# A four-layer graph network on one core: the first batch's opening chain by chunks, the order of the first loads, and the way in which column scales become rows

## The chip, the core and the metric

The kernel runs on one core of a Trainium2 chip. The metric is the device time of one execution in microseconds (us). The kernel before took 2319.86 us, the median of 3 runs (2318.74 to 2319.90).

The engines of the core are named as the profile names them: PE (matrix products; PEld is its load of the stationary operand), DVE (vector work), ACT (activation functions and copies), POOL (general work on the side, here mostly `x ** -0.5`), SP (here: the queue that starts the transfers). They run side by side, each through its own list of instructions in a fixed order, and wait for each other by semaphores. All data is float32.

## What is computed

For each of 32 batches there is a node matrix `x` of 512 x 128 and an adjacency matrix of 512 x 512. Four layers follow each other; each normalises its input, clips it at zero, and adds a graph network of that to the input:

```python
# layer 0
h = maximum(layernorm(x), 0)
d = sum(adj + I, axis=-1);  r = d ** -0.5
x = x + leaky_relu((r[:, None] * (adj + I) * r[None, :]) @ (h @ W) + b, 0.01)
# layer 1
h = maximum(layernorm(x), 0)
x = x + tanh(concat(adj @ elu(h @ W_in + b_in), elu(h @ W_node + b_node),
                    adj.T @ elu(h @ W_out + b_out)) @ W_upd + b_upd)
# layer 2: four inner layers over f, with the same two normalised matrices in all four
h = maximum(layernorm(x), 0)
A1 = adj / sqrt(sum(adj**2, axis=2));  A2 = adj / sqrt(sum(adj**2, axis=1))
f = tanh(concat(A1 @ (f@ws + bs), f@wn + bn, A2.T @ (f@wd + bd)) @ wu + bu)     # four times
x = x + f
# layer 3: a gated update (tanh of adj @ msg, then gates r, z, n)
```

What matters below: layer 0 can't start before the row sums of the batch's adjacency matrix and the mean and variance of its `x` are known. Layer 2 needs the square root of the sum of squares of each row and of each column of the matrix.

## The kernel before

A batch's matrix is held twice, as `a` (rows on the partitions, four chunks of 128 x 512) and as `aT` (its transpose). Instructions aren't written in the order in which they run. Every operation is recorded with an estimated duration, and a list scheduler (`Plan.order`) then fixes the order on every engine: among the operations that are ready it takes the one with the smallest key. The key comes from the batch's due time and the length of what still follows. A `rank` puts an operation ahead of all that have none. The estimates decide the order only; the hardware waits on semaphores.

```python
plan = Plan(sb, psum, {"bank": 8, "s2": 32, "s4": 6, "s8": 10}, {...})    # buffers of each size
o.key = (due - o.tail + o.later if o.rank is None else o.rank - 1e6, i)
def t_pow(n): return 0.9 + 0.1 * n          # estimate for the power on POOL
```

Where the plan expects PE to stand idle for over 0.7 us, it puts in products of the identity matrix with itself, into a bank that nobody uses ("idle products", tile `ps_idle`). They compute nothing that is needed[...].

```python
def kept_warm(self, done, product, begin):
    ...
        gap = o.ready - at
        if gap > self.SHORT:
            n = int(min(gap, cold) / self.COLD + max(gap - cold - 0.1, 0.0) / self.WARM)
```

The loads of the setup and of the first batch, with their ranks (a small one goes first). `raw` holds layer 2's weights, which the kernel multiplies together once at the start ("fold") so that the inner layers get by with fewer products:

```python
op("AQ", ..., w_sb[:, :D] ...)                      # layer 0's weight, on ACT's queue
op("AQ", ..., r_sb[:, :D] ...)                      # layer 0's bias, on ACT's queue
op("SP", 0.5, ... c_sb, bcol ..., rank=2)
op("SP", 0.5, ... w_sb[:, D:first] ..., rank=5)
op("SP", 0.5, spread(D, R_L3_MSG), ..., rank=5)
... raw[...] ..., rank=3 if i == 0 else 6           # three pieces: 768, 768 and 576 KB
def load(dst, src, kb, rank):                       # 4 pieces for batch 0, else 2
    ... rank=None if b else rank
op("SP", 0.4, ... xt.ap(), x[b] ..., rank=None if b else 0)
load(a, adj[b], 1024, 1)
load(aT, adjt[b], 1024, 4)
```

Layer 0's opening. `degree` sums the rows of `a` on ACT, the power is taken of all eight columns at once, and every chunk of `h` waits for all of it:

```python
def normed(xin, out_tag, extra=None):
    mv = moments(xin, v8)                                   # DVE: mean, variance of x
    if extra: extra(v8); n = 2 * NC                         # degree: row sums
    op("POOL", t_pow(n), ... inv[:, :n] = v8[:, :n] ** -0.5)
    op("DVE", 0.08, ... inv[:, at:at+NC] = inv[:, 0:NC] * inv[:, NC:2*NC])
    op("DVE", 0.08, ... nb = -mean * inv)
    for c in range(NC):
        op("ACT", ..., h[:, c, :] = relu(x[:, c, :] * inv[c] + nb[c]))

def degree(v8):
    for c in range(NC):
        op("ACT", 0.73, ... activation(sq, a[:, c, :], AF.Copy, accum_out=stat[:, c:c+1]))
    op("DVE", 0.08, ... v8[:, NC:] = stat + 1.0)

hr, inv0 = normed(xt, "h", degree)
def own(k, n):                                              # adds the identity to aT's own blocks
    nc.gpsimd.tensor_tensor(diag[:, k:k+n, :], blocks, ident..., op=ALU.add)
n = NC if b else 1
... op("POOL", ...)
psh = plan.bank("agg")                                      # then PE: aT and diag times h
```

After it come, for each batch, a copy of the aggregate (ACT), the product with layer 0's weight (`ps_lin`), `z`, `y` and the new `x` (DVE), the next normalisation, a transpose (`ps_t`), layer 1's two projections (`ps_sd`), their elu (`rep`, ACT and DVE), and layer 1's aggregation (`ps_agg<-aT,rep`).

Layer 2's scales. The sums of squares stand one for each partition; the multiplication of `aT` and `a` needs them along a row, the same on every partition. So they go to DRAM and come back spread over all partitions, as (node, scale), and ACT puts them into rows:

```python
inv = buf("inv", (P, 2 * NC))
op("POOL", t_pow(2 * NC), ... inv = stat ** -0.5)
bounce, spaced, rows = buf("bounce", (P, 2*NC)), buf("s4", (P, P, 2*NC), "spaced"), buf("s4", (P, 2, N), "rows")
op("SP", 0.4, bounced, [inv], [bounce], kb=128)             # 4 KB to DRAM
op("SP", 0.4, spread, [bounce], [spaced], kb=512)           # back, to every partition
op("ACT", t_act(2 * N), ... copy rows "p (s c) n" from spaced "p k n")
for s, m in enumerate((aT, a)):
    for c in range(NC):
        op("DVE", t_tt(N), ... m[:, c, :] = m[:, c, :] * rows[:, s, :])
```

Of the kernel before, what the change touches and what calls it, by code (L numbers as in the profile page):

```python
# [18 lines left out]
P = 128  # L19
# [5 lines left out]
PERIOD = 30.0  # L25
ENDING = 6.0
SMALL = 16


SEVEN = {"last": 0 * 5 * D, "mid": 1 * 5 * D, "gates": 2 * 5 * D}  # L30
# [9 lines left out]
W_L2 = []  # L40
# [219 lines left out]
def gnn_stack(  # L260
# [13 lines left out]
    sb = ctx.enter_context(tc.tile_pool(name="sb", bufs=1))  # L274
    psum = ctx.enter_context(tc.tile_pool(name="psum", bufs=1, space=bass.MemoryType.PSUM))
    dram = ctx.enter_context(tc.tile_pool(name="dram", bufs=1, space=bass.MemoryType.DRAM))
    plan = Plan(sb, psum, {"bank": 8, "s2": 32, "s4": 6, "s8": 10}, {"bank": 2, "s2": 5, "s4": 0, "s8": 1})

    w_sb = const.tile([P, W_COLS], F32, name="w_sb")
    c_sb = const.tile([P, C_COLS], F32, name="c_sb")  # L280
# [2 lines left out]
    cf_sb = const.tile([P, len(L2_CHUNKS)], F32, name="cf_sb")  # L283
    t_sb = const.tile([P, T_COLS], F32, name="t_sb")
    ident = const.tile([P, P], F32, name="ident")
    neg_half = const.tile([P, 2 * NC], F32, name="neg_half")

    def wt(col, n=D):
# [18 lines left out]
    def t_pool(n):  # L307
        return 0.15 + n / 450

    def t_pow(n):  # L310
        return 0.9 + 0.1 * n

    def op(*args, **kwargs):
        return plan.op(*args, **kwargs)

    def const_buf(name, ap):
        b = Buf(plan, name, name, None)
# [3 lines left out]
    W1, W2F, W3, CS, RS, RF, CF, TS, ID, NH = (const_buf(n, t) for n, t in (  # L321
        ("w1", w_sb), ("w2", w_sb), ("w3", w_sb), ("c_sb", c_sb), ("r_sb", r_sb), ("rf_sb", rf_sb),
        ("cf_sb", cf_sb), ("t_sb", t_sb), ("ident", ident), ("neg_half", neg_half)))

    def mm(ps, out_of, lhs, rhs, n, start, stop, reads, later=0.0):
        op("PE", t_mm(n), lambda: nc.tensor.matmul(out_of(ps.ap()), lhs(), rhs(), start=start, stop=stop),  # L326
# [10 lines left out]
    def setup():  # L337
# [1 line left out]

        op("POOL", 1.0, lambda: make_identity(nc, ident), [], [ID])  # L340
        op("POOL", 0.2, lambda: nc.gpsimd.memset(neg_half, -0.5), [], [NH])
        first = W_L2[0][0]

        def spread(lo, hi, to=None):
            return lambda: nc.sync.dma_start(
                r_sb[:, lo:hi] if to is None else to.ap()[:, :hi - lo], bass.AP(tensor=brow.tensor, offset=brow.offset + lo, ap=[[0, P], [1, hi - lo]]))
# [2 lines left out]
        op("AQ", 0.5, lambda: nc.scalar.dma_start(w_sb[:, :D], w[:, :D]), [], [(W1, {0})], kb=64)  # L349
        op("AQ", 0.5, lambda: nc.scalar.dma_start(  # L350
            r_sb[:, :D], bass.AP(tensor=brow.tensor, offset=brow.offset, ap=[[0, P], [1, D]])), [], [(RS, {0})], kb=64)
        op("SP", 0.5, lambda: nc.sync.dma_start(c_sb, bcol), [], [CS], kb=9, rank=2)
        op("SP", 0.5, lambda: nc.sync.dma_start(w_sb[:, D:first], w[:, D:first]), [], [(W1, {1})], kb=(first - D) / 2, rank=5)
        op("SP", 0.5, spread(D, R_L3_MSG), [], [(RS, {1})], kb=(R_L3_MSG - D) / 2, rank=5)
        op("SP", 0.5, spread(R_L3_MSG, R_COLS), [], [(RS, {2})], kb=(R_COLS - R_L3_MSG) / 2)
        hrz = plan.buf("s2", (P, N), "hrz")
        op("SP", 0.5, spread(R_L3_HRZ, R_L3_HRZ + 2 * D, hrz), [], [hrz], kb=D)
# [3 lines left out]
        for i in (0, 2, 3):  # L361
            lo, hi = RAW_L2[i][0], RAW_L2[i + 1][0] if i == 2 else RAW_COLS if i == 3 else RAW_L2[2][0]
            buf = plan.buf("s8", (P, NC, N), f"raw{i}")
            op("SP", 0.5, lambda buf=buf, lo=lo, hi=hi: nc.sync.dma_start(
                buf.ap().rearrange("p c n -> p (c n)")[:, :hi - lo], raw[:, lo:hi]), [], [buf], kb=(hi - lo) / 2, rank=3 if i == 0 else 6)
            raws += [(buf, lo)] * (2 if i == 0 else 1)
        op("SP", 0.5, lambda: nc.sync.dma_start(w_sb[:, W_L3_MSG:], w[:, first:]), [], [W3], kb=(W_COLS - W_L3_MSG) / 2)

        def block(i, col):
            buf, lo = raws[i]  # L370
# [48 lines left out]
    def program(b):  # L419
        plan.batch = b  # L420

        def buf(tag, shape=(P, N), name=None):
            return plan.buf(tag, shape, name)
# [10 lines left out]

        def load(dst, src, kb, rank):

            n = NC // pieces
            for k in range(pieces):
                s = slice(k * n, (k + 1) * n)
                op("SP", 0.4, lambda s=s: nc.sync.dma_start(dst.ap()[:, s, :], src[:, s, :]),  # L440
                   [], [(dst, set(range(NC)[s]))], kb=kb / pieces, rank=None if b else rank)

        op("SP", 0.4, lambda: nc.sync.dma_start(xt.ap(), x[b]), [], [xt], kb=256, rank=None if b else 0)
        load(a, adj[b], 1024, 1)
        load(aT, adjt[b], 1024, 4)

        def moments(xin, v8):
            st, mv = buf("bn", (P, NC, nc.vector.BN_STATS_DIM)), buf("mv", (P, NC, nc.vector.BN_AGGR_DIM))
            for c in range(NC):
                op("DVE", 0.193, lambda c=c: nc.vector.bn_stats(st.ap()[:, c, :], xin.ap()[:, c, :]), [xin], [(st, {c})])  # L450
            for c in range(NC):
                op("DVE", 0.066, lambda c=c: nc.vector.bn_aggr(mv.ap()[:, c, :], st.ap()[:, c, :]), [(st, {c})], [(mv, {c})])
            op("DVE", 0.08, lambda: nc.vector.tensor_scalar_add(v8.ap()[:, 0:NC], mv.ap()[:, :, 1], LN_EPS), [mv], [(v8, {0})])  # L453
            return mv

        def normed(xin, out_tag, extra=None):


            v8 = buf("v8", (P, 2 * NC))
            n = NC  # L460
            mv = moments(xin, v8)
            if extra:
                extra(v8)
                n = 2 * NC
            inv = buf("sc", (P, 3 * NC))
            op("POOL", t_pow(n), lambda: nc.gpsimd.tensor_tensor(inv.ap()[:, :n], v8.ap()[:, :n], neg_half[:, :n], op=ALU.pow),  # L466
               [v8, NH], [(inv, {0})])
            at = 0
            if extra:
                at = 2 * NC  # L470
                op("DVE", 0.08, lambda: nc.vector.tensor_mul(inv.ap()[:, at:at + NC], inv.ap()[:, 0:NC], inv.ap()[:, NC:2 * NC]),
                   [(inv, {0})], [(inv, {1})])
            nb = buf("nb", (P, NC))
            op("DVE", 0.08, lambda: nc.vector.scalar_tensor_tensor(nb.ap(), mv.ap()[:, :, 0], -1.0, inv.ap()[:, at:at + NC],  # L474
                                                                   op0=ALU.mult, op1=ALU.mult), [mv, inv], [nb])
            h = buf("s2", rows_shape, out_tag)
            for c in range(NC):
                op("ACT", t_act(D, 2), lambda c=c: nc.scalar.activation(  # L478
                    h.ap()[:, c, :], xin.ap()[:, c, :], AF.Relu, bias=nb.ap()[:, c:c + 1],
                    scale=inv.ap()[:, at + c:at + c + 1]), [xin, nb, inv], [(h, {c})])  # L480
            return h, inv
# [157 lines left out]
                    sq.ap(), a.ap()[:, c, :], AF.Copy, accum_out=stat.ap()[:, c:c + 1]), [(a, {c})], [sq, (stat, {c})])  # L639
            op("DVE", 0.08, lambda: nc.vector.tensor_scalar_add(v8.ap()[:, NC:], stat.ap(), 1.0), [stat], [(v8, {1})])  # L640

        hr, inv0 = normed(xt, "h", degree)

        diag = buf("s2", rows_shape, "diag")

        def own(k, n):
            t = aT.ap()
            blocks = bass.AP(tensor=t.tensor, offset=t.offset + k * (N + P), ap=[list(t.ap[0]), [N + P, n], [1, P]])
            nc.gpsimd.tensor_tensor(diag.ap()[:, k:k + n, :], blocks, ident[:, None, :].to_broadcast([P, n, P]), op=ALU.add)

        n = NC if b else 1
        for k in range(0, NC, n):
            op("POOL", t_pool(n * P), lambda k=k, n=n: own(k, n), [(aT, set(range(k, k + n))), ID], [(diag, set(range(k, k + n)))])
        psh = plan.bank("agg")
        for c in range(NC):
            for lo, hi in ((0, c * P), (c * P, (c + 1) * P), ((c + 1) * P, N)):
# [58 lines left out]
        for c in range(NC):  # L715
            for s, m in ((0, a), (1, aT)):
                op("ACT", 0.73, lambda c=c, s=s, m=m: nc.scalar.activation(
                    sq.ap(), m.ap()[:, c, :], AF.Square, accum_out=stat.ap()[:, s * NC + c:s * NC + c + 1]), [(m, {c})], [sq, (stat, {s * NC + c})])
        inv = buf("inv", (P, 2 * NC))
        op("DVE", 0.08, lambda: nc.vector.tensor_scalar_max(stat.ap(), stat.ap(), NORM_EPS * NORM_EPS), [stat], [stat])  # L720
        op("POOL", t_pow(2 * NC), lambda: nc.gpsimd.tensor_tensor(inv.ap(), stat.ap(), neg_half, op=ALU.pow), [stat, NH], [inv])
        bounce, spaced, rows = buf("bounce", (P, 2 * NC)), buf("s4", (P, P, 2 * NC), "spaced"), buf("s4", (P, 2, N), "rows")

        def bounced():
            bounce.tile = dram.tile([P, 2 * NC], F32, name=f"bounce_{b}", tag=f"bounce_{bounce.slot}", bufs=1)
            nc.sync.dma_start(bounce.tile, inv.ap())

        def spread():
            d = bounce.tile
            nc.sync.dma_start(spaced.ap().rearrange("p n k -> p (n k)"),  # L730
                              bass.AP(tensor=d.tensor, offset=d.offset, ap=[[0, P], [1, 2 * N]]))

        op("SP", 0.4, bounced, [inv], [bounce], kb=128)
        op("SP", 0.4, spread, [bounce], [spaced], kb=512)
        op("ACT", t_act(2 * N), lambda: nc.scalar.copy(  # L735
            rows.ap().rearrange("p s (c n) -> p (s c) n", c=NC), spaced.ap().rearrange("p n k -> p k n")), [spaced], [rows])
        for s, m in enumerate((aT, a)):
            for c in range(NC):
                op("DVE", t_tt(N), lambda m=m, c=c, s=s: nc.vector.tensor_mul(m.ap()[:, c, :], m.ap()[:, c, :], rows.ap()[:, s, :]),  # L739
                   [(m, {c}), rows], [(m, {c})])  # L740


        h2, _ = normed(x2, "h")
# [51 lines left out]
           N, [psm, (RS, {2})])  # L795
        psa = plan.bank("agg")
        aT2 = buf("s8", (P, NC, N), "aT2")
        load(aT2, adjt[b], 1024, None)
        aggregate(psa, msg, 0, aT2)
        mT = buf("s2", name="mT")  # L800
        op("ACT", t_act(N), lambda: nc.scalar.activation(mT.ap(), psa.ap(), AF.Tanh), [psa], [mT])
# [112 lines left out]
```

## Time and profile before

| | value |
|---|---|
| time, median of 3 runs | 2319.86 us |
| span of the profiled execution | 2319.2 us |
| ACT busy | 946.4 us (41%), 2018 instructions |
| POOL busy | 262.6 us (11%), 218 instructions |
| transfers of the 16 engines, mean | 87 GB/s, 200.82 MB in all |
| granted PE clock, mean over the span | 0.998 |

Busy times are of each engine by itself and overlap. A row of instruction groups has the line, engine and operation, then what is written and read with the shape, the count, the busy time in us and the mean in ns, and last the idle time just before with what ended it. In a timeline the first number is the start in us, the second the length of the merged piece, and "[idle before <-releaser]" is given where the engine stood still. PE's matrix products overlap each other in the pipeline: one of 128 columns is shown as 275 ns, yet eight that follow each other start 0.11 us apart. The idle products are counted in PE's busy time.

### The profile page before, as it was taken

How to read it: one execution, taken by the hardware profiler on the slowest of the kernel's cores; microseconds unless marked ns; L12 is line 12 of the kernel's file. 1: busy time of each engine (PE TensorE's matmuls, PEld its weight loads, DVE VectorE, ACT ScalarE, POOL GpSimd, SP SyncE). 2: the span in 40 equal slices, each digit the busy share in tenths (PEclk: the TensorE clock that was granted, in tenths of full speed). 3: DMA queues.
4: the chain of work that ended last, by engine and by line, in shares of the span. 5: the costliest groups of instructions: out<-in, count | busy, mean ns of one | idle time of the engine just before them, and what ended most of it. 6: DMA issues, size and time to landing. Idle time of an engine off the chain costs nothing.

```text
span 2319.2 us, 28279 instructions
## 1 busy us (share of the span) xinstructions
PE 2301.0 (99%) x9682; PEld 1446.3 (62%) x9682; DVE 1530.8 (66%) x4132; ACT 946.4 (41%) x2018; POOL 262.6 (11%) x218
## 2 busy tenths in 40 slices
PE   9999999999999999999999999999999999999998
PEld 7656666666666566666666666666666666656665
DVE  5655666666667676676766676766766666767655
ACT  7323344334443344443344433444433444334412
POOL 3001101011111011010111101110101111101101
PEclk9999999999999999999999999999999999999999
DMA  7102332233222232222332322322223322223200
GB/s 261 46 10 64 105 94 75 81 101 107 76 91 82 82 109 81 87 79 86 105 100 83 91 82 82 109 81 88 78 86 105 107 76 91 82 82 105 77 6 27
DMA packets 133054, 200.82 MB, mean 87 GB/s; under 512 B 18992, under 2 KB 79920, under 8 KB 132912
## 3 DMA queue, kind: packets, MB, share of 16 engines
q1 hardware_dynamic: 132624, 198.90, 28.0%
q8 instruction: 76, 1.25, 0.2%
q14 instruction: 66, 0.54, 0.1%
q10 hardware_dynamic: 288, 0.13, 0.0%
HBM read 160.05 MB, written 38.93 MB: 86 GB/s over the span
## 4 chain that ended last, share of the span: by engine, by line
PE 91%; DMA 3%; DVE 3%; ACT 2%; POOL 1%; SPq 0%; issue 0%; DVEq 0%; ACTq 0%; POOLq 0%
PE ps_agg L326 61%; PE ps_seven L597 11%; PE ps_sd L326 9%; PE ps_upd L326 4%; PE ps_gate L326 2%; PE ps_msg L326 1%; DMA f4r<-turn_f4r 1%; PE ps_node L326 1%; PE ps_lin L326 1%; ACT h L478 1%; DMA turn_f4r<-blk 1%; POOL sc L466 1%; SPq L496 0%; ACT f L768 0%; DVE bn L450 0%
## 5 line engine op out<-in xcount | busy, mean ns | idle before, releaser
L326 PE MATMUL ps_agg<-aT,sd 128*128 128x512 f32 x1024 | 510.5, 594 | 0.1
L326 PE MATMUL ps_agg<-a,sd 128*128 128x512 f32 x1024 | 482.4, 592 | 0.0
L466 POOL TENSOR_TENSOR sc<-v,neg_half 128x4 f32<-128x4 f32 (+1 forms) x128 | 157.8, 1233 | 1638.6 <-DVE v L453 1361.8
L326 PEld LDWEIGHTS ps_agg<-a,sd 128*128 128x128 f32 x1024 | 184.6, 190 | 182.8 <-issue 178.4
L326 PE MATMUL ps_agg<-f,w_sb 128*128 128x512 f32 x448 | 229.6, 594 | 3.9 <-ACT f L768 3.8
L326 PEld LDWEIGHTS ps_agg<-aT,sd 128*128 128x128 f32 x1024 | 177.7, 191 | 83.0 <-issue 66.7
L326 PE MATMUL ps_sd<-w_sb,f 128*128 128x256 f32 x768 | 217.4, 380 | 0.5 <-ACT f L768 0.4
L478 ACT ACTIVATE h<-xr,nb,sc 128x128 f32<-128x128 f32 x384 | 158.2, 482 | 136.4 <-DVE nb L474 136.3
L597 PEld LDWEIGHTS ps_seven<-t_sb,s 128*128 128x128 f32 x1128 | 161.6, 191 | 78.1 <-issue 69.3
L326 PEld LDWEIGHTS ps_sd<-w_sb,f 128*128 128x128 f32 x768 | 136.6, 191 | 95.2 <-issue 76.5
L597 PE MATMUL ps_seven<-t_sb,s 128*128 128x128 f32 x1128 | 168.1, 275 | 0.0
L735 ACT COPY rows<-spaced 128x1024 f32<-128x1024 f32 x32 | 66.1, 2064 | 164.9 <-DMA spaced<-bounce 164.9
L326 PE MATMUL ps_agg<-aT,rep 128*128 128x512 f32 x256 | 131.3, 596 | 2.1 <-DVE rep L693 2.1
L326 PE MATMUL ps_agg<-a,rep 128*128 128x512 f32 x256 | 131.3, 596 | 0.0
L768 ACT ACTIVATE f<-ps_agg,cf_sb 128x512 f32<-128x512 f32 x128 | 87.2, 682 | 98.8 <-PE ps_agg L326 98.8
L326 PE MATMUL ps_agg<-aT,msg 128*128 128x512 f32 x256 | 124.9, 592 | 0.0
L487 DVE STREAM_TRANSPOSE blk<-f 128x512 f32<-128x512 f32 x29 | 20.6, 711 | 144.2 <-ACT f L768 144.2
L326 PE MATMUL ps_agg<-aT,h 128*128 128x256 f32 (+2 forms) x384 | 99.3, 381 | 0.2 <-ACT h L478 0.2
L597 PEld LDWEIGHTS ps_seven<-w_sb,f 128*128 128x128 f32 x512 | 75.9, 191 | 35.4 <-issue 27.7
L739 DVE TENSOR_TENSOR aT<-aT,rows 128x512 f32<-128x512 f32 x128 | 87.9, 687 | 14.7 <-PE ps_agg L326 14.6
L553 DVE TENSOR_TENSOR sd<-ps_sd,rf_sb 128x512 f32<-128x512 f32 x128 | 86.9, 679 | 15.5 <-PE ps_sd L326 15.4
L739 DVE TENSOR_TENSOR a<-a,rows 128x512 f32<-128x512 f32 x128 | 88.1, 689 | 13.6 <-PE ps_agg L326 13.5
(144 smaller groups left out, 3817.3 us busy)
## 6 DMA issues: line engine op xcount, KB each, us to landing
aT<-in_adjt SPq DMA_DIRECT2D x124, 512.0 KB, 5.2
a<-in_adj SPq DMA_DIRECT2D x62, 512.0 KB, 5.2
turn_turned<-blk SPq DMA_DIRECT2D x348, 64.0 KB, 1.8
turned<-turn_turned SPq DMA_DIRECT2D x87, 256.0 KB, 2.6
spaced<-bounce SPq DMA_DIRECT2D x32, 512.0 KB, 4.0
x<-in_x SPq DMA_DIRECT2D x32, 256.0 KB, 2.8
out<-xo SPq DMA_DIRECT2D x30, 256.0 KB, 2.0
turn_f4r<-blk SPq DMA_DIRECT2D x116, 64.0 KB, 1.8
```

Of the source, the lines that this page charges most:

```text
L326: op("PE", t_mm(n), lambda: nc.tensor.matmul(out_of(ps.ap()), lhs(), rhs(), start=start, stop=stop), reads, [ps], later=later)
L466: op("POOL", t_pow(n), lambda: nc.gpsimd.tensor_tensor(inv.ap()[:, :n], v8.ap()[:, :n], neg_half[:, :n], op=ALU.pow), [v8, NH], [(inv, {0})])
L478: op("ACT", t_act(D, 2), lambda c=c: nc.scalar.activation(h.ap()[:, c, :], xin.ap()[:, c, :], AF.Relu, bias=nb.ap()[:, c:c + 1], scale=inv ...
L487: op("DVE", t_tt(N), lambda: nc.vector.transpose(blk.ap().rearrange("p b (c r) -> p c b r", c=NC), m.ap().rearrange("p c (b s) -> p c b s" ...
L553: op("DVE", t_tt(N), lambda ps=ps, h=h: nc.vector.tensor_add(sd.ap()[:, 2 * h:2 * h + 2, :], ps.ap().rearrange("p (j v) -> p j v", j=2), s ...
L597: op("PE", t_mm(D), lambda j=j: nc.tensor.matmul(ps.ap()[:, k * H + j * D:k * H + (j + 1) * D], lhs()[:, j * P:(j + 1) * P], rhs(), start= ...
L735: op("ACT", t_act(2 * N), lambda: nc.scalar.copy(rows.ap().rearrange("p s (c n) -> p (s c) n", c=NC), spaced.ap().rearrange("p n k -> p k ...
L739: op("DVE", t_tt(N), lambda m=m, c=c, s=s: nc.vector.tensor_mul(m.ap()[:, c, :], m.ap()[:, c, :], rows.ap()[:, s, :]), [(m, {c}), rows], [ ...
L768: op("ACT", t_act(N, 1), lambda ps=ps, i=i, f_new=f_new: nc.scalar.activation(f_new.ap(), ps.ap(), AF.Tanh, bias=cf_sb[:, i:i + 1]), [ps, ...
```

## The change

There are four parts.

1. **First batch by chunks.** Batch 0 gets a version of the opening of layer 0 in which the row sum of each chunk of `a` is taken by DVE as soon as that chunk is there, and the power, the scale and the chunk of `h` follow chunk by chunk. The identity is added to `aT`'s own blocks by DVE instead of POOL for batches 0 and 1.
2. **Ranks.** One list, `FIRST`, ranks all loads of the start: batch 0's `x`, `a`, `aT` ahead of the small bias columns, the raw weights and the rest, and the loads of batches 1 and 2 right after those.
3. **Layer 2's scales.** DVE transposes the scales in 32 x 32 blocks before they go to DRAM, so that 32 neighbouring nodes of one scale lie side by side. They then come back in an order that the multiplication can read in place. The copy on ACT and the buffer `spaced` are gone. For this the scales stand in constant buffers 32 columns wide.
4. **Plan.** The estimate of the power on POOL becomes `0.35 + 0.157 * n`; there is one buffer less of size s4 and one more of size s2; the plan counts batch 0's `a` at twice its size.

```diff
+TURN = 32
+OWN = 2
+FIRST = ["x0", "a0", "aT0", "c", "raw0", "w1", "r1", "raw2", "raw3", "x1", "a1", "aT1", "x2", "a2", "aT2"]
-    plan = Plan(sb, psum, {"bank": 8, "s2": 32, "s4": 6, "s8": 10}, ...)
+    plan = Plan(sb, psum, {"bank": 8, "s2": 33, "s4": 5, "s8": 10}, ...)
     def t_pow(n):
-        return 0.9 + 0.1 * n
+        return 0.35 + 0.157 * n
+    INV, INV_T = ([const_buf(f"inv{j}_{k}", inv_sb[:, 4 * j + k, :]) for k in range(4)] for j in range(2))
+        op("POOL", 0.21, lambda: nc.gpsimd.memset(inv_sb, 0.0), [], INV + INV_T)
... (in load, and in the setup's loads alike)
+            name = f"{rank}{b}"
+            rank, kb = first(name), kb * (2 if name == "a0" else 1)
...
+        def normed_by_chunk(xin, out_tag):
+            mv = moments(xin, v8)
+            op("POOL", t_pow(NC), ... inv[:, :NC] = v8[:, :NC] ** -0.5)
+            for c in range(NC):
+                op("DVE", t_tt(N), ... nc.vector.tensor_reduce(stat[:, c:c + 1], a[:, c, :], AX.X, ALU.add))
+                op("DVE", 0.08, ... v8[:, at:at + 1] = stat[:, c:c + 1] + 1.0)
+                op("POOL", t_pow(1), ... inv[:, at:at + 1] = v8[:, at:at + 1] ** -0.5)
+                op("DVE", 0.08, ... inv[2 * NC + c] = inv[c] * inv[NC + c])
+                op("DVE", 0.08, ... nb[c] = -mean * inv[2 * NC + c])
+                op("ACT", t_act(D, 2), ... h[:, c, :] = relu(x[:, c, :] * inv[2 * NC + c] + nb[c]))
-        hr, inv0 = normed(xt, "h", degree)
+        hr, inv0 = normed_by_chunk(xt, "h") if b < 1 else normed(xt, "h", degree)
-            nc.gpsimd.tensor_tensor(diag.ap()[:, k:k + n, :], ...)
+            own_engine.tensor_tensor(diag.ap()[:, k:k + n, :], ...)
+        own_engine, own_name = (nc.vector, "DVE") if b < OWN else (nc.gpsimd, "POOL")
...
-        inv = buf("inv", (P, 2 * NC))
+        inv, turned_inv = INV[b % len(INV)], INV_T[b % len(INV_T)]
-        bounce, spaced, rows = buf("bounce", (P, 2 * NC)), buf("s4", (P, P, 2 * NC), "spaced"), buf("s4", (P, 2, N), "rows")
+        bounce, rows = buf("bounce", (P, TURN)), buf("s4", (P, NC, 2, NC, TURN), "rows")
+        op("DVE", 0.1, lambda: nc.vector.transpose(turned_inv.ap(), inv.ap()), [inv], [turned_inv])
-            nc.sync.dma_start(spaced..., bass.AP(..., ap=[[0, P], [1, 2 * N]]))
+            nc.sync.dma_start(rows..., bass.AP(..., ap=[[0, P], [TURN * TURN, NC], [1, 2 * P]]))
-        op("ACT", t_act(2 * N), lambda: nc.scalar.copy(... rows from spaced ...))
         for s, m in enumerate((aT, a)):
             for c in range(NC):
-                op("DVE", t_tt(N), ... tensor_mul(m[:, c, :], m[:, c, :], rows[:, s, :]))
+                op("DVE", t_tt(N), ... tensor_mul(m[:, c, :] as "p k q r", the same,
+                    rows.ap()[:, :, s].rearrange("p q c r -> p c q r")))
```

## The prediction, made before the change was run

> **What bounds the kernel now.** I read the engine totals first, then the PE groups with shapes kept apart, then the timelines of PE, ACT, DVE and POOL over the first 47 us, then the waits.
>
> ```profile
> PE 2301.0 (99%) x9682; PEld 1446.3 (62%) x9682; DVE 1530.8 (66%) x4132; ACT 946.4 (41%) x2018; POOL 262.6 (11%) x218
> L864 PE MATMUL ps_idle<-ident 128*128 128x128 f32 x120 | 17.3, 309 | 1.4 <-POOL ident masks.py:199 1.4
> ```
>
> PE is busy for 2301.0 of 2319.2 us, and the change takes no needed product away from it. So time can only come from where PE stands still or runs idle products: 18.2 us of idleness and 17.3 us of idle products, 35.5 us or 1.5% in all. By stretches of the span, from 100 to 2200 us PE is busy for 2095.5 of 2100 us with 8 idle products. What can be gained lies in the start and, less so, in the end. The start, by PE's timeline:
>
> ```profile
> 1.40 9.48 PE L864 MATMUL ps_idle<-ident 128*128 128x128 f32 x58 [1.40 <-POOL ident masks.py:199]
> 11.14 1.57 PE L326 MATMUL ps_fold<-raw 128*128 128x128 f32 x12 [0.27 <-DMA raw<-in_raw]
> 13.66 0.46 PE L326 MATMUL ps_agg<-diag,h 128*128 128x128 f32 x2 [0.94 <-ACT h L478]
> ...
> 24.07 3.37 PE L864 MATMUL ps_idle<-ident 128*128 128x128 f32 x28
> 27.27 1.35 PE L514 MATMUL ps_t<-ident,h 128*128 128x128 f32 x4
> 28.46 1.50 PE L864 MATMUL ps_idle<-ident 128*128 128x128 f32 x12
> ...
> 36.46 1.13 PE L326 MATMUL ps_agg<-aT,rep 128*128 128x512 f32 x2 [2.10 <-DVE rep L693]
> ```
>
> The first needed product starts at 11.14 us. Lost before 36.46 us: 11.14 to that point, 0.94 waiting for `h`, 3.20 (24.07 to 27.27) and 1.34 (28.46 to 29.80) in idle products, 0.23 for a chunk of `h`, and 2.10 for `rep`: **18.95 us**. So PE has done 36.46 - 18.95 = 17.5 us of needed work when layer 1's aggregation of batch 0 starts. From then on it hardly waits. The chain that sets this start is batch 0's alone, and the other engines show four delays in it:
>
> ```profile
> 9.22 0.63 ACT L638 ACTIVATE sq<-a 128x512 f32<-128x512 f32 x1
> 13.03 1.63 ACT L478 ACTIVATE h<-x,nb,sc 128x128 f32<-128x128 f32 x4
> 31.14 2.06 ACT L735 COPY rows<-spaced 128x1024 f32<-128x1024 f32 x1 [0.89 <-DMA spaced<-bounce]
> ```
>
> ```profile
> 25.33 1.23 DVE L474 SCALAR_TENSOR_TENSOR nb<-mv,sc 128x4 f32<-128x4 f32 x1 [0.18 <-POOL sc L466]
> 34.15 1.53 DVE L691 TENSOR_SCALAR rep<-rep 128x512 f32<-128x512 f32 x1 [1.73 <-ACT rep L690]
> ```
>
> ```profile
> 10.23 1.65 POOL L466 TENSOR_TENSOR sc<-v,neg_half 128x8 f32<-128x8 f32 x1 [8.89 <-DVE v L640]
> 25.27 1.27 POOL L649 TENSOR_TENSOR diag<-aT,ident 128x512 f32<-128x512 f32 x1
> 34.13 1.26 POOL L649 TENSOR_TENSOR diag<-aT,ident 128x512 f32<-128x512 f32 x1 [5.87 <-DMA aT<-in_adjt]
> ```
>
> The last row sum starts at 9.22, the power of eight columns ends at 11.88, and `h` begins at 13.03. The copy of `rows` holds ACT when `rep` would be next (`rep` starts at 33.50, though DVE had the first half of `sd` at 31.56). Twice a DVE instruction takes 1.1 us longer than its like (`nb` has a mean of 168 ns, this `rep` step 440 ns), each time beside POOL's addition of the identity.
>
> **What the Trainium skill says.** "SBUF — State Buffer", section "Who interferes with whom": VectorE and GpSimd share a pair of ports, which one of them holds for a whole instruction; a reduction doesn't take it. The trace agrees with the blocking: 1.23 and 1.53 us above. "DMA: Bandwidth & Descriptors", section "Queues, rings and completion order": each transfer engine takes its queue's descriptors in order, but transfers needn't complete in the order of issue over all engines. The trace agrees roughly: by 9.1 us, when batch 0's last piece of `a` lands, some 2.1 MB have moved though only 1.4 MB were issued up to it. "TensorE: Matmul & The Clock Gate", section "What's actually happening": an idle window lowers the clock. The trace has a granted clock of 0.87 from 36.4 to 50 us, after the wait of 2.10 us.
>
> **The parts and their cost.**
>
> *Ranks.* `raw0` (768 KB) now goes behind `aT`. Before, `a`'s pieces land at 5.4, 6.5, 8.3 and 9.1 us, `raw0` at 11.0, and `aT`'s pieces from 11.6 to 13.5. From 8 to 16 us transfers run at 373 to 441 GB/s. `a` has nothing less ahead of it and stays at about 9. `aT`'s last piece has 768 KB less: at 410 GB/s that is 1.9 us, so 11.6. `raw0` lands at about 13.5.
>
> *Chunks.* Last chunk at 9.1; row sum on DVE 0.65 (my estimate, as any 128x512 step: 0.68); addition 0.16; one-column power: 1.65 us for eight and 1.09 for four give 0.14 a column and an estimated 0.67 for one; two small steps 0.33; `h` 0.48. That makes 11.4 us for the last chunk of `h`, where the four ended at 14.66. With `aT` at 11.6, diag on DVE 0.28 and the last chunk's three products (0.93 us), the aggregation ends at 12.9 instead of 17.39: **4.5 us earlier**. It now follows the arriving chunks instead of starting after them. Its own work of 3.73 us is the same.
>
> *From there to layer 1's aggregation.* Before: 36.46 - 17.39 = 19.1 us. Out of it go 1.1 (`nb`, since batch 1's identity is added by DVE, for 0.6 us elsewhere), and up to 1.9 for `rows` on ACT. The second block of 1.1 is batch 2's, still on POOL, and goes only if it falls elsewhere. Against this, batch 0 waits behind other work on ACT (squares, 0.73 us each) and DVE as before, and PE's folds now come later, from 13.5 us. I take 2.5 to 3 us off. The start of layer 1's aggregation is then near 12.9 + 16.4 = **29.3 us** instead of 36.46.
>
> *What PE loses then.* The folds (66 products 0.11 us apart, 7.3 us), batch 0's aggregation (3.73), `ps_lin` (0.91), the transpose (0.45), `ps_sd` (1.72) and layer 1's node product (0.86) are 15.0 us and all ready before 29.3. Batch 1's first products give perhaps 0.7 more, since its matrix still comes after all weights. Lost: 29.3 - 15.7 = 13.6 instead of 18.95: **5.4 us gained**. A full loss of PE's 7.2 us isn't recovered, because 1.8 us of batch 1's work move behind that point.
>
> *Clock.* 13 percent of 13.6 us was 1.8 us; if the wait for `rep` gets shorter, some of it returns. I count 0.5.
>
> *Steady state.* For each batch ACT loses a copy of 2.07 us (66.1 in 32) and DVE gains a small transpose (estimate 0.15 us, 5 in 32). The multiplications read their rows in runs of 32; the addition of `f4r` already does that and takes 690 ns, as much as the plain form at 687 to 689. The way back from DRAM has runs of 1 KB instead of 4 KB: perhaps 4 to 5 us instead of 4.0. None of this is on PE. PE waits for ACT's `f` for 3.8 us in all, and ACT without the copies may take 1 us of that. I count 0.8.
>
> Sum: 5.4 + 0.5 + 0.8 = 6.7 us; 2319.86 - 6.7 = **2313.2 us**.
>
> **Rivals.** *(a) The transfers become the bound of the start.* They are above 370 GB/s almost throughout from 8 to 22 us, and batch 1's and 2's matrices come after 5.1 MB of other loads. If PE reaches batch 1's work earlier but its matrix isn't there, the lead is lost again to a later wait. For: batch 2's addition waits 5.87 us for `aT`. Against: before, SP stood still for 14.6 us with loads behind it, and the ranks put those ahead.
>
> ```profile
> SPq L726 <- POOL inv L721: 20.9, 2, 14.6
> ```
>
> Gain 2 to 3 us, time near 2317. *(b) The new order fits badly.* Estimates and buffer counts change every engine's order over all 32 batches, and the tail (36 us after 2283, where DVE steps end the run) is sensitive to it; a poor fit costs 1 to 3 us. Time 2316 to 2321. *(c) Everything on the chain goes.* Both blocks and the whole 1.9 us leave, layer 1's aggregation starts at 27, and batch 1 is in time: 8 to 10 us, time 2310 to 2312. *(d) DVE becomes the bound.* It is at 66% and gets 5 us more: no effect is expected; strided multiplications would have to take over twice as long.
>
> **Range and chances.** (a) and (b) pull up, (c) down, at about equal weight. Range 2308.5 to 2318.0. Even all idle products and idleness of the start are 19 us, 0.8%, so over 2% (46 us) either way can't come from these steps: within 2% 0.985, faster 0.005, slower 0.01 for a mistake in the order that I don't see.
>
> **What would show it.** Right: PE's aggregation of batch 0 starts near 10 and ends near 13 us; the first fold product comes after it or within it; layer 1's aggregation starts between 27 and 31; idle products fall by some 20 or more; no `rows` copy on ACT; multiplications remain near 0.69 us; PE's loss from 100 to 2200 us remains below 5 us. Wrong: a new wait of PE for `aT`, `h` or `rep` of batches 1 or 2 between 30 and 60 us (rival a), an end after the last product longer than before (rival b), or multiplications near 1 us.

## The result, and the profile after

The changed kernel takes **2378.9 us** (median of 6 runs) where the kernel before takes 2319.88: a ratio of 1.025, with a 95% interval of 1.0233 to 1.0267. It is 59 us slower. The prediction was 2313.2 us with a range to 2318.0.

First the page of the changed kernel: the engine totals, the idle products (from the PE groups), and the one group in which the difference shows at once.

```profile
PE 2314.3 (97%) x9670; PEld 1450.6 (61%) x9670; DVE 1549.9 (65%) x4182; ACT 876.4 (37%) x1978; POOL 255.1 (11%) x218
L907 PE MATMUL ps_idle<-ident 128*128 128x128 f32 x108 | 14.7, 294 | 1.4 <-POOL ident masks.py:199 1.4
L336 PE MATMUL ps_agg<-f,w_sb 128*128 128x512 f32 x448 | 238.3, 615 | 40.4 <-ACT f L811 40.4
```

The same group in the kernel before:

```profile
L326 PE MATMUL ps_agg<-f,w_sb 128*128 128x512 f32 x448 | 229.6, 594 | 3.9 <-ACT f L768 3.8
```

The last column is the idle time just before the group, with what ended it. PE waits 40.4 us for ACT's `f`; before, it was 3.8 us. It is idle for 2377.9 - 2314.3 = 63.6 us instead of 18.2. It is also busy for 13.3 us longer with the same needed products. The mean granted clock is 0.995 instead of 0.998, which is some 7 us of the span (estimate: 0.003 of 2378), and the group above has a mean of 615 ns instead of 594. The loss isn't at the start, which went much as intended:

```profile
1.40 7.72 PE L907 MATMUL ps_idle<-ident 128*128 128x128 f32 x54 [1.40 <-POOL ident masks.py:199]
10.35 0.46 PE L336 MATMUL ps_agg<-diag,h 128*128 128x128 f32 x2 [1.24 <-DVE diag L689]
13.92 1.28 PE L907 MATMUL ps_idle<-ident 128*128 128x128 f32 x10
...
24.07 1.06 PE L907 MATMUL ps_idle<-ident 128*128 128x128 f32 x8
...
27.63 1.73 PE L907 MATMUL ps_idle<-ident 128*128 128x128 f32 x14
30.43 1.12 PE L336 MATMUL ps_agg<-aT,rep 128*128 128x512 f32 x2 [1.08 <-DVE rep L734]
```

Layer 1's aggregation of batch 0 starts at 30.43 us, 6 us earlier than before. The loss is spread over the whole steady part: from 100 to 2300 us PE is busy for 2150.5 us of 2200, where it was 2195.1. One such place shows how it arises. In the changed kernel's timelines of SP, DVE, ACT and PE, in this order:

```profile
561.31 0.40 SPq L774 DMA_DIRECT2D rows<-bounce  x1
562.66 0.34 SPq L540 DMA_DIRECT2D f4r<-turn_f4r  x1
```

```profile
568.39 0.69 DVE L827 TENSOR_TENSOR xr<-xr,f4r 128x512 f32<-128x512 f32 x1 [2.54 <-DMA f4r<-turn_f4r]
...
573.02 0.16 DVE L514 SCALAR_TENSOR_TENSOR nb<-mv,sc 128x4 f32<-128x4 f32 x1
```

```profile
573.22 1.65 ACT L518 ACTIVATE h<-xr,nb,sc 128x128 f32<-128x128 f32 x4 [2.38 <-DVE nb L514]
574.78 0.67 ACT L811 ACTIVATE f<-ps_agg,cf_sb 128x512 f32<-128x512 f32 x1
```

```profile
575.50 1.13 PE L336 MATMUL ps_agg<-f,w_sb 128*128 128x512 f32 x2 [2.34 <-ACT f L811]
```

`f4r` is the turned result of layer 2. Its transfer is issued 1.35 us behind the spread of the scales, and DVE can use it only at 568.39. DVE stands still for it for 2.54 us. Everything behind it in DVE's fixed order is late, `nb` too; ACT waits for `nb` with `h` at the head of its own order; and `f` of another batch, for which PE is waiting, stands behind that `h`. Two engines pass a late transfer on to PE. The table of transfers (KB each, median us from issue to landing) shows that both got slower; the first two lines are of the changed kernel, the last three of the kernel before.

```profile
rows<-bounce SPq DMA_DIRECT2D x32, 512.0 KB, 5.4
f4r<-turn_f4r SPq DMA_DIRECT2D x29, 256.0 KB, 4.8
```

```profile
spaced<-bounce SPq DMA_DIRECT2D x32, 512.0 KB, 4.0
f4r<-turn_f4r SPq DMA_DIRECT2D x29, 256.0 KB, 3.3
turned<-turn_turned SPq DMA_DIRECT2D x87, 256.0 KB, 2.6
```

The same 512 KB now come in runs of 1 KB instead of 4 KB (145345 packets in all instead of 133054, that is 12291 more; three more for each of 128 partitions in 32 batches make 12288). It takes 1.4 us longer, and `f4r` behind it 1.5 us. What DVE waits for `f4r` over the whole run, in the changed kernel and in the kernel before:

```profile
L827 DVE TENSOR_TENSOR xr<-xr,f4r 128x512 f32<-128x512 f32 x29 | 20.0, 691 | 45.7 <-DMA f4r<-turn_f4r 45.7
```

```profile
L784 DVE TENSOR_TENSOR xr<-xr,f4r 128x512 f32<-128x512 f32 x29 | 20.0, 690 | 13.5 <-DMA f4r<-turn_f4r 12.5
```

### The profile page after: what moved, and what is told of

Read it like the earlier page. It is cut to its first block, busy times and chain, and to the rows that moved or that the text cites. A ratio compares the mean times of both kernels' runs of the same rounds, so it can differ in the third digit from the quotient of the medians.

```text
span 2377.9 us, 28318 instructions
## 1 busy us (share of the span) xinstructions
PE 2314.3 (97%) x9670; PEld 1450.6 (61%) x9670; DVE 1549.9 (65%) x4182; ACT 876.4 (37%) x1978; POOL 255.1 (11%) x218
## 2 busy tenths in 40 slices
DMA packets 145345, 201.23 MB, mean 85 GB/s; under 512 B 18993, under 2 KB 96305, under 8 KB 145201
## 4 chain that ended last, share of the span: by engine, by line
PE 72%; DMA 10%; DVE 10%; ACT 4%; SPq 2%; POOL 1%; issue 1%; POOLq 0%; ACTq 0%; DVEq 0%
PE ps_agg L336 50%; PE ps_seven L637 7%; PE ps_sd L336 7%; DMA f4r<-turn_f4r 5%; PE ps_upd L336 3%; DMA turn_f4r<-blk 2%; PE ps_gate L336 2%; ACT h L518 2%; DVE blk L527 2%; ACT f L811 1%; SPq L536 1%; POOL sc L506 1%; DVE bn L464 1%; PE ps_msg L336 1%; PE ps_node L336 1%
## 5 line engine op out<-in xcount | busy, mean ns | idle before, releaser
L506 POOL TENSOR_TENSOR sc<-v,neg_half 128x4 f32<-128x4 f32 (+1 forms) x127 | 149.6, 1179 | 1727.1 <-DVE v L467 1375.5
L336 PE MATMUL ps_agg<-f,w_sb 128*128 128x512 f32 x448 | 238.3, 615 | 40.4 <-ACT f L811 40.4
L336 PEld LDWEIGHTS ps_agg<-aT,sd 128*128 128x128 f32 x1024 | 172.7, 191 | 78.6 <-issue 44.7
L637 PEld LDWEIGHTS ps_seven<-t_sb,s 128*128 128x128 f32 x1128 | 164.9, 193 | 67.8 <-issue 58.4
L336 PE MATMUL ps_agg<-aT,rep 128*128 128x512 f32 x256 | 126.4, 593 | 1.8 <-DVE rep L734 1.8
L336 PE MATMUL ps_agg<-a,rep 128*128 128x512 f32 x256 | 126.0, 592 | 0.0
L678 ACT ACTIVATE sq<-a 128x512 f32<-128x512 f32 x124 | 77.7, 626 | 119.7 <-DMA a<-in_adj 118.0
L336 PEld LDWEIGHTS ps_agg<-f,w_sb 128*128 128x128 f32 x448 | 77.1, 194 | 65.2 <-ACT f L811 45.4
```

Of the source, the lines that this page charges most:

```text
L637: op("PE", t_mm(D), lambda j=j: nc.tensor.matmul(ps.ap()[:, k * H + j * D:k * H + (j + 1) * D], lhs()[:, j * P:(j + 1) * P], rhs(), start= ...
L678: op("ACT", 0.73, lambda c=c: nc.scalar.activation(sq.ap(), a.ap()[:, c, :], AF.Copy, accum_out=stat.ap()[:, c:c + 1]), [(a, {c})], [sq, ( ...
```

## The experiments

Theory R: short runs make the spread slow, and `f4r` behind it carries the delay through DVE and ACT to PE. Rival O: the new order of instructions is worse in itself. The experiments were run in four groups.

**Run length.** Only the shape in which the spread is read changes; the order of every engine stays. (e2 has three more small issues on SP for each batch.)

```diff
 e1 (changed kernel)   -ap=[[0, P], [TURN * TURN, NC], [1, 2 * P]]   +ap=[[0, P], [1, 2 * N]]
 e5 (changed kernel)   -ap=[[0, P], [TURN * TURN, NC], [1, 2 * P]]   +ap=[[0, P], [TURN * TURN // 2, 2 * NC], [1, P]]
 e3 (kernel before)    -ap=[[0, P], [1, 2 * N]]                      +ap=[[0, P], [0, NC], [1, 2 * P]]
 e2 (changed kernel, scales compact in DRAM)
-nc.sync.dma_start(bounce.tile, turned_inv.ap())
+for q in range(NC):
+    nc.sync.dma_start(bounce.tile[q], turned_inv.ap()[q * TURN:q * TURN + 2 * NC, :])
-ap=[[0, P], [TURN * TURN, NC], [1, 2 * P]]
+ap=[[0, P], [1, 2 * N]]
```

e1: 

> The changed kernel with one thing undone: the scales come back from DRAM in one run of 4 KB for each partition instead of four of 1 KB. Same bytes, same order of all instructions; the rows then hold the wrong scales, so the output isn't the reference's. Theory R (the short runs make this transfer slow, 5.4 instead of 4.0 us, the transfer of f4r behind it lands late, at 4.8 instead of 3.3 us, and VectorE, ScalarE and at last TensorE wait in their fixed order): the transfer back to 4.0 us, f4r near 3.3, TensorE's wait for f below 8 us in all, time 2310 to 2322 us. Rival O (the new fixed order and buffer counts leave too little beside the waits, whatever the transfer takes): f4r may fall, but the time stays at 2365 us or more.

e2: 

> The changed kernel, with the scales written to DRAM by four small transfers of 8 partitions each, so that the 4 KB that are needed lie together and come back in one run for each partition. It computes the reference. Theory R: as the run with the 4 KB runs, 2310 to 2322 us, the three more small issues hidden. Rival O: 2365 us or more.

e5: 

> The changed kernel with the scales coming back in eight runs of 512 bytes instead of four of 1 KB (other, wrong scales; the output isn't the reference's). Same bytes, same order. Theory R: the transfer takes some 2 to 3 us longer still, about 8 us, f4r lands at 7 or later, and the time rises further, to 2420 us or more. Rival O: within 10 us of 2379.

e3: 

> The kernel before, with one thing added: the scales come back in four runs of 1 KB for each partition (the first 1 KB four times, so the scales are wrong and the output isn't the reference's). Same bytes, same order as before. Theory R: the transfer goes from 4.0 to about 5.4 us, f4r from 3.3 to about 4.8, time 2350 to 2380 us. Rival O: 2318 to 2326 us, since the old order is kept.

| run | order | runs | spread lands, us | `f4r` lands, us | DVE waits for `f4r`, us in all | time, us | ratio to before |
|---|---|---|---|---|---|---|---|
| before | old | 4 KB | 4.0 | 3.3 | 12.5 | 2319.9 | 1 |
| e3 | old | 1 KB, the same one four times | 8.3 | 7.4 | 126.5 | 2505.8 | 1.0798 (1.0782 to 1.0814) |
| e1 | new | 4 KB | 4.1 | 3.4 | 13.1 | 2337.8 | 1.008 (1.0065 to 1.0095) |
| e2 | new | 4 KB, compact | not listed | not listed | 16.0 | 2341.6 | 1.0092 (1.0075 to 1.0109) |
| changed | new | 1 KB | 5.4 | 4.8 | 45.7 | 2378.9 | 1.025 (1.0233 to 1.0267) |
| e5 | new | 512 B | 5.8 | 5.1 | 56.1 | 2399.2 | 1.0344 (1.0321 to 1.0367) |

"Not listed" means that the profile of this run gives no landing times. In the new order the time follows the landing of `f4r`. The shape of the read explains 2378.9 - 2341.6 = 37 us in a kernel that computes the same. But theory R had promised 2322 at most, and 18 to 22 us of loss stay at 4 KB: R isn't the whole. Two sizes were off: halving the runs once more adds 0.4 us to the spread and not 2 to 3, so e5's time stays below the 2420 us of theory R; in e3 the spread took 8.3 and not 5.4 us. There all packets read the same 1 KB of DRAM, which the changed kernel doesn't. And in the old order the spread is also what ACT's copy waits for (297.6 us in e3 instead of 164.9). So e3 shows that late transfers cost time in the old order too, but neither what 1 KB runs cost nor what `f4r` costs by itself. One thing these runs don't separate: with the runs' length their distance in DRAM changes too (1 KB out of every 4 KB, 512 bytes out of every 2 KB, or 4 KB in one piece).

**The parts of the change one by one.** What is left could come from the new estimate of the power (theory P), or from the new scales or the start (rival S).

```diff
 g1 = e2, and              -return 0.35 + 0.157 * n   +return 0.9 + 0.1 * n
 g6 = kernel before, and   -return 0.9 + 0.1 * n      +return 0.35 + 0.157 * n
 g4 = kernel before with normed_by_chunk, FIRST and OWN = 2 alone (and the plan counts batch 0's a at twice its size)
 g7 = kernel before with the scales of e2, and s2: 33, s4: 5
```

g1: 

> The changed kernel with the compact 4 KB runs (2341.6 us) and the old estimate of the power, 0.9 + 0.1 n, in the plan. Only the fixed order differs from the compact kernel. Theory P (what is left of the loss comes from the new estimate: it gives 0.98 us for four columns where the chip takes 1.03 to 1.09, so the order has no slack behind POOL): 2312 to 2322 us, TensorE's waits in the steady part about as before. Rival S (it comes from the new way of the scales itself or from the start): 2335 us or more.

g6: 

> The kernel before with the new estimate of the power alone. Theory P: 2330 to 2345 us. Rival S: within 4 us of 2319.

g4: 

> The kernel before with the first batch by chunks and the ranks alone; scales, estimate and buffer counts as before. If the start brings what the prediction says and nothing else goes wrong: 2312 to 2317 us. If the remaining loss of the compact kernel comes from the start's new phase: 2330 us or more.

g7: 

> The kernel before with the scales turned by VectorE, written compactly and read in place from 4 KB runs, and the buffer counts of the change; no chunks, no ranks, the old estimate. Theory P: 2314 to 2322 us. Rival S: 2335 us or more.

| run | time, us | ratio to before |
|---|---|---|
| g4, start alone | 2318.6 | 0.9986 (0.9979 to 0.9993) |
| g7, scales alone, 4 KB | 2320.9 | 0.9999 (0.999 to 1.0008) |
| g6, estimate alone | 2346.4 | 1.011 (1.0093 to 1.0127) |
| g1, start and scales, old estimate | 2327.6 | 1.0029 (1.0018 to 1.004) |

The start brings about 3 us, a little less than expected. The scales bring nothing by themselves. The estimate, which changes no needed instruction but only the order, costs 25 us alone (1.4 us more than theory P's range), so theory P holds as to the part. Yet g1 at 2327.6 is neither's number: start and scales together cost 6 us although neither does alone. Where the scales' copies are gone, ACT just waits elsewhere. Of g7, then of the kernel before:

```profile
ACT h L483 <- DVE nb L479: 375.0, 95, 9.2
```

```profile
ACT h L478 <- DVE nb L474: 144.1, 73, 8.2
```

That is 230.9 us more waiting for `nb`, as much as the copies had taken (66.1) and waited for the spread (164.9).

**`f4r` out of the way.** If a late `f4r` is the cause, then it must help to let it go first, with the spread as slow as it is. In g10 the two neighbours in SP's order are exchanged in 26 batches; DVE, ACT, PE and POOL keep their order; the traces of the changed kernel and of g10 have the same sequence on each of them.

```diff
+        for s in self.spreads:              # at the end of Plan.order
+            i = done.index(s)
+            j = next((k for k in range(i + 1, len(done)) if done[k].engine == "SP"), None)
+            if j is not None and done[j] in self.f4rs:
+                done.insert(j, done.pop(i))
 g8 (changed kernel, estimates only)
-op("SP", 0.4, spread, [bounce], [rows], kb=512)      +... kb=682
-... [bounce], [mT], kb=256                           +... kb=577 if name == "f4r" else 256
```

g10: 

> The changed kernel with its 1 KB runs, and one thing moved: the transfer that spreads the scales starts just after the transfer of f4r instead of just before it (26 batches). Every other engine keeps its order; the output is the reference's. Theory R (the loss comes from f4r standing behind a slow transfer, not from the scales being late): f4r lands after 2.6 to 3 us, VectorE's wait for it below 20 us in all, time 2332 to 2345 us, though the scales come at 6 us or later. Rival L (the scales themselves are late): 2375 us or more.

g8: 

> The changed kernel with its 1 KB runs; only the plan's estimates differ: the spread of the scales counted at 5.4 us to landing, f4r at 4.8, as measured in the changed kernel. The data and instructions are the same, in another order. If the loss comes from an order made on wrong estimates: 2335 to 2355 us. If the later landing can't be hidden by any order of this plan: 2370 us or more.

g10 takes **2327.1 us** (ratio 1.0024, 1.0013 to 1.0035), less than theory R's range. The exchange alone takes 51.8 us off. Its transfers, then its step on DVE with the idle time for `f4r`, and PE's wait for `f`:

```profile
rows<-bounce SPq DMA_DIRECT2D x32, 512.0 KB, 5.1
...
f4r<-turn_f4r SPq DMA_DIRECT2D x29, 256.0 KB, 2.7
```

```profile
L835 DVE TENSOR_TENSOR xr<-xr,f4r 128x512 f32<-128x512 f32 x29 | 19.9, 688 | 2.3 <-DMA f4r<-turn_f4r 2.2
L342 PE MATMUL ps_agg<-f,w_sb 128*128 128x512 f32 x448 | 229.8, 595 | 1.6 <-ACT f L819 1.6
```

The spread is still slow and starts later, and nothing is lost by it: rival L falls. The gain is larger than the 37 us of the read's shape, since `f4r` behind a spread of 4 KB runs was late too in the new order (the last 14.5 us: e2 to b3 below). g8 (2364.8 us, ratio 1.019, 1.0173 to 1.0207) fell between its two numbers. Its order, too, has `f4r` landing after 2.7 us, yet PE gets 282 idle products instead of 108 and waits 15.8 us for `sd`. True numbers for two transfers gave another order with other waits, so g8 doesn't tell how much a better plan could hide.

**A square, and the version to keep.** All with start, new scales and `f4r` first, or (b1) start and old scales.

```diff
 b1 = g4 + the exchange        b2 = g1 + the exchange        b3 = e2 + the exchange
 b5 = g10, and   -return 0.35 + 0.157 * n   +return 0.9 + 0.1 * n
```

b1: 

> The version that should beat both: first batch by chunks and ranks (2318.6 us alone), scales, estimate and buffers as in the kernel before, and the spread of the scales started just after f4r's transfer instead of just before it in 26 batches. If f4r behind the spread costs the old order something too (VectorE waits 12.5 us for it there): 2310 to 2316 us. If it is hidden there, or the copy of the rows on ScalarE now comes late: 2318 us or more.

b2: 

> Chunks and ranks, the scales turned by VectorE and read in place from compact 4 KB runs, the old estimate (2327.6 us so far), and f4r's transfer ahead of the spread. If what is left of that loss is f4r behind the spread: 2312 to 2320 us. If it has another cause: 2324 us or more.

b3: 

> As the version at 2313.0 us, but with the new estimate of the power: compact 4 KB runs and f4r ahead of the spread. If the new estimate costs time only because its order leaves no slack for f4r: 2311 to 2317 us. If it costs time by itself, through other waits (VectorE's sd, 6 us in the changed kernel): 2323 to 2330 us.

b5: 

> As the version at 2313.0 us, but with the change's own way back, four runs of 1 KB: old estimate, f4r ahead of the spread. If short runs cost only what stands behind them in the queue: 2311 to 2317 us. If they cost time by themselves: 2323 us or more.

| time, us | new estimate | old estimate |
|---|---|---|
| 1 KB runs, spread first | 2378.9 (changed) | not run |
| 4 KB runs, spread first | 2341.6 (e2) | 2327.6 (g1) |
| 1 KB runs, `f4r` first | 2327.1 (g10) | **2313.0** (b5) |
| 4 KB runs, `f4r` first | 2327.1 (b3) | **2313.0** (b2) |

The two lower rows are alike: with `f4r` first, run length costs nothing. With 4 KB runs the exchange is worth 14.5 us under the new estimate and 14.6 under the old one, so the 6 us that g1 lost were `f4r` behind the spread. The columns differ by 14.0 or 14.1 us in all three rows that were run in both: that is the estimate's own share here. So theory R and rival O each hold for a part: the transfers' order costs the larger one, the order on the other engines the smaller one. Both 2313.0 versions beat both kernels, b2 with a ratio of 0.9966 (0.9954 to 0.9979) and b5 with 0.997 (0.9958 to 0.9981); b5 is the change as it stands, less the estimate and with two transfers exchanged in 26 batches. In b5, PE is idle for 2312.0 - 2296.8 = 15.2 us in all.

```profile
PE 2296.8 (99%) x9664; PEld 1444.0 (62%) x9664; DVE 1532.9 (66%) x4182; ACT 881.6 (38%) x1978; POOL 256.8 (11%) x218
```

Where do the 14.1 us go? The orders with the new estimate have a wait in common that PE's weight load shows, for the inner layers' `sd`. In the waits (us in all, times, longest) of b3, g6, the kernel before and b5:

```profile
PEld ps_agg L342 <- DVE sd L601: 25.8, 30, 1.5
```

```profile
PEld ps_agg L326 <- DVE sd L553: 22.9, 31, 1.5
```

```profile
PEld ps_agg L326 <- DVE sd L553: 7.2, 14, 0.9
```

```profile
PEld ps_agg L342 <- DVE sd L601: 6.0, 11, 0.9
```

About once per batch the new order puts too little between the product `ps_sd` and the aggregation that reads it. The wait marks a place and doesn't add up to the 14.1 us: the weight load waits while PE is still busy with earlier products, and PE's own idle time for `sd` is 5.7 us in b3. In g6 PE also waits 15.1 us for `f` instead of 3.8, which goes with the larger loss of 25 us there. Why an estimate for POOL has that effect, and whether a closer one would, was not tried; that the estimate is too small is not shown (0.98 us for four columns, 1.03 measured in b3).

b1 was a miss: 2343.7 us, ratio 1.0106 (1.009 to 1.0121), slower than g4 without the exchange. PE's wait for `f` in b1 (5.2 us in g4), then ACT's copy in b1 and in g4:

```profile
PE ps_agg L340 <- ACT f L814: 21.9, 26, 2.4
```

```profile
L781 ACT COPY rows<-spaced 128x1024 f32<-128x1024 f32 x32 | 66.0, 2061 | 204.4 <-DMA spaced<-bounce 204.4
```

```profile
L773 ACT COPY rows<-spaced 128x1024 f32<-128x1024 f32 x32 | 66.0, 2063 | 172.6 <-DMA spaced<-bounce 172.6
```

There the spread goes on to ACT's copy of 2.06 us. ACT waits 204.4 us for the spread instead of 172.6, and `f` stands behind the copy: once per batch, up to 2.4 us. In g10, b2 and b5 DVE, which now reads the scales itself, waits 2.0 us for them at most in the whole run. So in these runs the exchange pays where hardly any engine waits for the scales in its order. That is what the new scales buy: alone they give nothing, but they make the spread a transfer that may be late.

## Why the prediction was wrong, point by point

**The step that failed** is in the paragraph on the steady state: "The way back from DRAM has runs of 1 KB instead of 4 KB: perhaps 4 to 5 us instead of 4.0. None of this is on PE." The size was nearly right (5.4 us). The conclusion wasn't. The transfer's own data isn't urgent, but `f4r`, issued 1.35 us behind it, is, and it lands late behind it: after 4.8 us, and after 2.7 when it is issued ahead of the spread (g10). Taking it out of the way is worth 51.8 us in the changed order. My own sign for this part, PE's loss from 100 to 2200 us below 5 us, stood at 49.2. The place could have been seen in the trace of before: `f4r` (256 KB) landed after 3.3 us there and `turned` (another turned result of the same size) after 2.6. I asked what the copies' end would give to PE, and not who stands behind the longer transfer. In the Trainium skill, "DMA: Bandwidth & Descriptors", section "Queues, rings and completion order", says that each transfer engine takes its queue's descriptors in order. I used it only for the start; it leads to that question, and the 4.8 and 2.7 us agree with it.

**The second** is rival (b), the order, at 1 to 3 us. The estimate's share alone is 14.1 us with `f4r` out of the way, and 25 us in the old kernel. That the estimate was nearer to the measured mean on POOL said nothing about the order that comes out.

**The bound on the loss** failed with them. I limited both directions by the 19 us that the start holds. That limits a gain and not a loss: with PE busy for 99% of the time, a new wait on it has almost no idle time to vanish in.

**Ranks** were right within half a us: the last of `aT`'s blocks gets its identity at 11.94 without a wait for its transfer, so it had landed by then; 11.6 was expected.

**Chunks** were right in kind. The aggregation's copy starts at 14.12 us where it was 17.42, so 3.3 us earlier instead of 4.5. The last chunk of `h` runs at 12.35 instead of 10.9, since its row sum came behind an addition of the identity on DVE, and it came behind a square on ACT.

**To layer 1's aggregation:** 16.3 us from the copy (16.4 expected), start at 30.43 instead of 29.3. Lost before it: 10.35, then 13.92 to 15.35, 24.07 to 24.97 and 27.63 to 30.43, in all 15.5 us (13.6 expected, 18.95 before). Both blocks by POOL's addition left this chain: batch 2's (1.55 us from 31.22) now stretches DVE's `node` step from 0.69 to 1.76 us, behind that point. A wait of 1.89 us for batch 2's `h` follows at 43.9. Its step on DVE, at 42.51, stands behind batch 0's multiplications, and these had waited 2.19 us for the scales, which took 8.4 us to DRAM and 6.3 us back among the loads. That is rival (a) on a small scale, but by the scales and not by a matrix.

**Clock:** granted 1.00 from 36.4 to 50 us instead of 0.87, worth 1.8 us where I counted 0.5; but over the whole span it fell, from 0.998 to 0.995.

**Multiplications** in place: 0.69 us, as expected. The transpose takes 0.21 us, 6.7 in all. ACT's 66 us turned into other waits of ACT.

**The sum** of 6.7 us looks as if it came out in b5, which is 2319.95 - 2313.02 = 6.9 us faster. That is in part luck, since the terms are others. The start (5.4 and 0.5 expected) brought 2.8 us alone in g4. In b5 PE loses 15.1 us before layer 1's aggregation instead of 18.95, and 1.9 of the gain go again in the wait for batch 2's `h`. From 100 to 2200 us PE is busy for 3.5 us more (0.8 expected), with an exchange of transfers that the prediction doesn't have. From the changed kernel, the exchange takes 51.8 us off and then the old estimate 14.1, which leaves the gain of 6.9: 51.8 + 14.1 - 6.9 = 59.0 us, the whole loss. In another order of undoing the shares would differ, as the estimate's 25 us in the old kernel show.

## What to carry to other kernels

When a transfer gets slower, don't only ask who needs its data: look at what is issued just behind it on the queue, and on which engine's fixed order that lands. Where an engine is 99% busy in a fixed order, an upper bound on a gain says nothing about the loss, and a change of a scheduler's estimate is a change of the kernel. Before dropping a change that lost, undo its parts one by one: here the chunks, the ranks and the new scales are all in the fastest version (chunks and ranks were not run apart).

## What the runs showed of the hardware that was not expected

- 512 KB spread from 4 KB of DRAM to 128 partitions, issued ahead of `f4r`, land after 4.0 to 4.2 us in one run of 4 KB (before, e1, g4, g6), 5.4 in runs of 1 KB (changed) and 5.8 in runs of 512 bytes (e5); the larger step is between 4 KB and 1 KB. The distance of the runs in DRAM changes with their length.
- In the old order, 512 packets that all read the same 1 KB took 8.3 us to land (e3). Why, the runs don't tell.
- 256 KB issued about 1.35 us behind such a spread land after 3.3 us where the spread takes 4.0, 4.8 where it takes 5.4, 5.1 where it takes 5.8 and 7.4 where it takes 8.3; issued ahead of it they land after 2.6 to 2.7 us.
- A power on POOL takes 0.55 us for one column, 1.02 to 1.09 for four and 1.64 to 1.67 for eight, each the mean of a group (before, changed, b3, b5).
